# First sweep of a four-layer graph network: the additions to the adjacency tiles moved from VectorE to accumulating transfers

## The chip, the cores and the metric

The kernel runs on one core of a Trainium2 chip. The metric is the device time of one execution in microseconds. A profile comes from one further execution of the same program, in which the hardware profiler records every instruction and every transfer.

## The reference

`x` has 2708 rows of 512 features, `adj` is 2708 x 2708 with about 1% of random positive entries and a filled diagonal. Four layers, each followed by a layer norm of `x + layer(x)`:

```python
# layer 0: row-normalised mask added to the adjacency
mask = adj > 0
head = mask / max(sqrt(sum(mask*mask, -1)), 1e-12)
inc = adj + head
y0 = (inc @ x) / sum(inc, -1)
# layer 1: attention on the adjacency, and a plain graph convolution, each with a gate
x_a = softmax-like(exp(-leaky(s_left + s_right)) where adj != 0) @ (x @ W_sa)
y1 = sigmoid(attn_a * x_a + attn_b * (adj @ (x @ W_gcnb) + b))
# layer 2: x@w0 + A x@w1 + A A x@w2 + A A A x@w3
# layer 3: relu((a_norm @ x + x) @ W + b)
```

The change concerns layer 0 alone: `inc = adj + mask / sqrt(degree)`, element by element.

## The kernel before

All arithmetic is in fp32 on the transposed adjacency `adjT`, so that a tile has 128 source nodes as partitions and up to 384 target nodes as columns. The matrix is seen as 2 x 2 quadrants of 1354 rows ("11", "12", "21", "22"), and products with it are formed by a seven-product scheme: sums of quadrants (`comb`, L403, in place or into a tile `s3`) and sums of feature blocks (`x_sums`, `x_last`) go into seven matmul groups P1 to P7 (`step`, L458) instead of eight.

A sweep passes over all target columns once. There are seven, begun at `S[0]` to `S[6]`; the first one, `S[0]`, is layer 0. It takes its columns in four ranges, `RANGES0 = [(768, 256), (0, 384), (384, 384), (1024, 330)]` (start and width within a half). The first of them is "plain", with eight products and no sums of quadrants. The three later ranges are what the diff calls later. In each range 40 tiles of 128 rows (10 for each quadrant) and four tiles of the rest come in: for each half a tile `r` of 116 partitions (74 rows of the first half, 42 of the second) and a tile `r32` of 128 partitions, which holds the last 32 rows four times.

For each tile of the first sweep `prepare` or `rest_prepare` calls `prep0` before the tile is used. `prep0` has two VectorE instructions: L769 writes `t = (a > 0) * row`, with `row` the inverse roots of the degrees of this range's columns, spread over all partitions; L770 adds `t` to `a`. After that `comb` forms the sums of quadrants, `add_run` (L765) adds up the row sums that divide the result at the end, and the matmuls read the tiles.

`row` must be known before a range begins. So while one range runs, the tiles of the next are read a first time (`count_load`, L698 into tiles `cl`; its transfers carry L149 and L151, the lines of `move`), turned into 0/1 masks by ScalarE (`count_mask`, L712, L713), and added up by small matmuls (`count_tile`, L723). These first reads are issued by POOL's queue, except those of the range (0, 384), which SyncE issues. POOL's queue also stores the finished rows of the layer (`store`) and loads the next sweep's features, and POOL computes the reciprocal root of each layer norm (L560). The tiles themselves are loaded by SyncE (`load`, L394).

Buffers: adjacency tiles, the products `t` (the profile calls them s) and `s3` share one ring of `RING = 38` buffers; `tmp` has 17, from which `cl`, `row` and the sums come; masks have 6.

The order of the work is a list of (position, function) pairs, put in with `at` and sorted by position. A range is seven units long; for a range that begins at `pb`, quadrant 11 is loaded from `pb - 1`, 21 from `pb - 0.4`, 22 from `pb + 0.75`, 12 from `pb + 3.2`, and `prep0` follows each load by 0.3 units or more:

```python
when = {"11": (-1.0, 1.0), "21": (-0.4, 1.0), "22": (0.75, 0.8), "12": (3.2, 1.0)}
cw = {"s3": 0.3, "s1": 1.25, "s2": 2.1, "s4": 4.3}
pw = {ij: (p + 0.3, f) for ij, (p, f) in when.items()}
```

From the sorted list the framework's planner gives each engine its order of instructions, with costs of its own, and assigns buffers as they come free in its plan. The list's order is pinned on the engines at the beginning (positions under `START = 5.0`) and for the pieces put in with `hold`. Each engine, and each engine's transfer queue, then works strictly in its order, waiting on semaphores.

Of the kernel before, what the change touches and what calls it, by code (L numbers as in the profile page):

```python
# [24 lines left out]
ALU = mybir.AluOpType  # L25
# [5 lines left out]
RANGES0 = [(768, 256), (0, 384), (384, 384), (1024, 330)]  # L31
# [37 lines left out]
def gnn_kernel(ctx: ExitStack, tc: tile.TileContext, x, adjT, w_sa, a_sa, w_gcn, b_gcn, wab, bab, w_hop, w_out,  # L69
               b_out, out):  # L70
    nc = tc.nc
# [87 lines left out]
    def trans(nm):  # L159
        return pool.tile([P, 384], F32, name=nm, tag="ring", bufs=RING)  # L160
# [606 lines left out]
    def prep0(R0, n, h, col, w, a):  # L767
        t = trans("s")
        nc.vector.scalar_tensor_tensor(t[:w, :n], a[:w, :n], 0.0, row[R0, h][:w, :n], ALU.is_gt, ALU.mult)  # L769
        nc.vector.tensor_tensor(a[:w, :n], a[:w, :n], t[:w, :n], ALU.add)  # L770

    def run_sums(R0, n, h, after):

# [82 lines left out]
    for k in range(KW):  # L856
# [6 lines left out]
        at(7.5 + f, lambda k=k: x_last(k))  # L863
    at(9.3, start0)
    sweep(S[0], RANGES0, prep=prep0, extra=extra0, done=done0, first=True, sums=True)


# [510 lines left out]
    for i in range(4):  # L1378
        for g, p in enumerate((S[2] + 19.3 + 1.1 * i, S[3] + 6.6 + 1.3 * i)):
            a = ({}, g, i // 2, i % 2)  # L1380
# [220 lines left out]
```

## Time and profile before

| | |
|---|---|
| median of 3 runs | 2888.12 us (2884.0 to 2891.57) |
| the profiled execution | 2883.33 us, of which 2881.2 us are its span |
| TensorE busy | 2832.7 us, 98% of the span |
| VectorE busy | 2195.9 us, 76% |
| ScalarE, POOL busy | 550.1 us, 617.6 us |
| TensorE's granted clock | 0.998 of full speed |
| L769, mask times inverse root | 132 in the later ranges, 67.3 us |
| L770, the addition | 132 in the later ranges, 67.6 us; the last at 393.1 us |
| transfers | 510.04 MB, 177 GB/s over the span |

Times are counted from the start of the span. The later ranges' tiles are prepared between 103 and 394 us. An fp32 matmul leaves two records in the trace, one after the other; the records of TensorE are pipelined and their ends are modelled, so a row of TensorE that is full says that it was never seen empty. In a table by stages each engine has its busy time and the number of its instructions, and at the end stand TensorE's granted clock, the busy share of the 16 DMA engines and the GB/s that they moved. In the issue lists a queue with the name software_dynamic is POOL's.

### The profile page before, as it was taken

The page shows a single profiled execution, that of the slowest core. Times are in us where ns is not written, and L with a number is a line of the kernel's source. Part 1 is how long each engine was busy: PE and PEld are TensorE (multiplying, and loading weights), DVE is VectorE, ACT ScalarE, POOL GpSimd, SP SyncE. Part 2 cuts the span into 40 slices and gives each one's busy share as a digit, 9 for nine tenths or more (in the row PEclk, how much of TensorE's full clock was granted, in tenths as well). Part 3 has the DMA queues.
Part 4 walks back from the last instruction along what each step waited for, and adds up shares of the span by engine and source line. Part 5 has one row for each costly group of instructions (what it writes and reads, how often), then busy time and mean ns, then how long its engine had stood idle before and what let it go on. Part 6 is the DMA issues. An engine that isn't in the chain of part 4 may idle for free. (4 is left out here: it accounts for less than half of the span.)

```text
span 2881.2 us, 37482 instructions
## 1 busy us (share of the span) xinstructions
PE 2832.7 (98%) x10963; PEld 1870.3 (65%) x10963; DVE 2195.9 (76%) x5670; ACT 550.1 (19%) x1119; POOL 617.6 (21%) x1113
## 2 busy tenths in 40 slices
PE   7999999999999999999999999999999999999998
PEld 5655665657765656866666666666666666666665
DVE  6898798576736464654699787887878877799987
ACT  4544200111136444542100000000000100100001
POOL 0123223123320101122203123031230211501202
PEclk9999999999999999999999999999999999999999
DMA  7665466354544333565667767566675666754542
GB/s 229 193 212 179 133 204 218 124 181 143 183 140 130 117 113 98 151 198 151 195 205 236 213 192 246 166 201 208 187 250 168 181 197 182 230 174 145 175 142 92
DMA packets 368524, 510.04 MB, mean 177 GB/s; under 512 B 63424, under 2 KB 321700, under 8 KB 368320
## 3 DMA queue, kind: packets, MB, share of 16 engines
q1 hardware_dynamic: 302392, 370.56, 43.5%
q0 software_dynamic: 49344, 126.38, 13.1%
q10 hardware_dynamic: 16584, 10.71, 1.3%
q8 instruction: 87, 1.43, 0.2%
q14 instruction: 117, 0.96, 0.1%
HBM read 423.77 MB, written 83.65 MB: 176 GB/s over the span
## 5 line engine op out<-in xcount | busy, mean ns | idle before, releaser
L1212 DVE TENSOR_TENSOR z<-z 128x339 f32<-128x339 f32 (+1 forms) x966 | 454.3, 503 | 12.5 <-PE accu L1267 3.2
L1285 ACT COPY q<-accu 128x338 f32<-128x338 f32 (+1 forms) x84 | 34.6, 443 | 1003.3 <-PE accu L1267 806.0
L560 POOL TENSOR_TENSOR rstd<-rstd,neg_half 128x1 f32<-128x1 f32 (+3 forms) x91 | 59.3, 652 | 762.2 <-DVE rstd L559 516.6
L1267 PE MATMUL accc<-s,t 128*128 128x338 f32 (+1 forms) x644 | 198.1, 450 | 0.0
L1267 PE MATMUL accu<-z,t 128*128 128x338 f32 (+1 forms) x644 | 194.0, 448 | 1.5 <-DVE z L1212 1.5
L1267 PE MATMUL accd<-z,t 128*128 128x338 f32 (+1 forms) x644 | 193.9, 448 | 0.6 <-DVE q L1349 0.6
L1267 PE MATMUL accc<-z,t 128*128 128x338 f32 (+1 forms) x644 | 193.5, 448 | 0.5 <-ACT q L1285 0.5
L1400 POOL DMA_DIRECT2D Y<-y x192 | 105.1, 554 | 366.3 <-DVE y L1395 333.3
L403 DVE TENSOR_TENSOR a<-a,a 128x384 f32<-128x384 f32 (+2 forms) x330 | 162.4, 510 | 23.1 <-PE accu L458 22.4
L1267 PEld LDWEIGHTS accc<-s,t 128*128 128x128 f32 x644 | 120.9, 190 | 64.1 <-issue 7.5
L1267 PEld LDWEIGHTS accc<-z,t 128*128 128x128 f32 x644 | 122.0, 190 | 61.6 <-issue 1.0
L1267 PEld LDWEIGHTS accu<-z,t 128*128 128x128 f32 x644 | 121.7, 190 | 61.7 <-DVE z L1212 2.0
L1267 PEld LDWEIGHTS accd<-z,t 128*128 128x128 f32 x644 | 121.9, 190 | 60.5 <-DVE q L1349 1.5
L1212 DVE TENSOR_TENSOR s<-z 128x338 f32<-128x338 f32 (+1 forms) x322 | 149.7, 503 | 12.7 <-PE accc L1267 8.4
L1291 DVE TENSOR_TENSOR q<-q,accd 128x338 f32<-128x338 f32 (+1 forms) x112 | 56.0, 500 | 115.2 <-PE accd L1267 115.2
L1068 DVE SCALAR_TENSOR_TENSOR a<-a,e 128x384 f32<-128x384 f32 (+2 forms) x160 | 77.4, 507 | 49.8 <-ACT e L1067 49.5
L1066 ACT ACTIVATE e<-row,s_right 128x384 f32<-128x384 f32 (+5 forms) x176 | 96.3, 569 | 76.2 <-PE accc L458 20.4
L965 DVE SCALAR_TENSOR_TENSOR deg<-a,deg 128x384 f32<-128x384 f32 (+2 forms) x152 | 75.2, 505 | 19.0 <-DMA a<-in_adjT 17.9
L406 POOL DMA_DIRECT2D As<-a x120 | 64.9, 544 | 82.3 <-DVE a L403 80.3
L1067 ACT ACTIVATE e<-e 128x384 f32<-128x384 f32 (+5 forms) x176 | 79.3, 477 | 1.8
L606 PE MATMUL ps_d<-w,xT 128*128 128x512 f32 (+1 forms) x176 | 79.2, 593 | 0.4 <-ACT xT L597 0.4
L769 DVE SCALAR_TENSOR_TENSOR s<-a,row 128x384 f32<-128x384 f32 (+2 forms) x152 | 75.0, 505 | 6.0 <-ACT row L754 6.0
(683 smaller groups left out, 5869.0 us busy)
## 6 DMA issues: line engine op xcount, KB each, us to landing
z<-As SPq DMA_DIRECT2D x320, 169.5 KB
z<-As SPq DMA_DIRECT2D x320, 169.0 KB
a<-in_adjT SPq DMA_DIRECT2D x240, 192.0 KB
z<-in_adjT SPq DMA_DIRECT2D x240, 169.5 KB
z<-in_adjT SPq DMA_DIRECT2D x240, 169.0 KB
a<-in_adjT SPq DMA_DIRECT2D x120, 165.0 KB
a<-in_adjT SPq DMA_DIRECT2D x112, 128.0 KB
As<-a POOLq DMA_DIRECT2D x60, 192.0 KB, 4.2
```

What stands on the lines that cost most here:

```text
L403: nc.vector.tensor_tensor(A[r, dst, k][:, :n], A[r, a, k][:, :n], A[r, b, k][:, :n], op)
L406: nc.gpsimd.dma_start(out=SD[m][k * P : (k + 1) * P, R0 : R0 + n], in_=A[r, dst, k][:, :n])
L560: nc.gpsimd.tensor_tensor(rstd[:w, 1:2], rstd[:w, 0:1], neg_half[:w], ALU.pow)
L606: nc.tensor.matmul(o, lhs(c), r, start=c == 0 and n == 0, stop=c == DC - 1, skip_group_check=True)
L769: nc.vector.scalar_tensor_tensor(t[:w, :n], a[:w, :n], 0.0, row[R0, h][:w, :n], ALU.is_gt, ALU.mult)
L965: nc.vector.scalar_tensor_tensor(d[:w, :n], a[:w, :n], 0.0, d[:w, :n], ALU.not_equal, ALU.add)
L1066: nc.scalar.activation(e[:w, :n], row[R0, h][:w, :n], AF.Prelu, bias=s_right[:w, t : t + 1], alpha=0.01)
L1067: nc.scalar.activation(e[:w, :n], e[:w, :n], AF.Exp, scale=-1.0)
L1068: nc.vector.scalar_tensor_tensor(a[:w, :n], a[:w, :n], 0.0, e[:w, :n], ALU.not_equal, ALU.mult)
L1212: nc.vector.tensor_tensor(d[:, :n], Z[x + (k,)][:, :n], Z[y + (k,)][:, :n], op)
L1267: nc.tensor.matmul(B[home][:, :n], stat(v, k), a[:, :n], start=bool(start and k == 0), stop=k == nk - 1, skip_group_check=True)
L1400: nc.gpsimd.dma_start(out=rows[:, :, f * P : (f + 1) * P], in_=o[32 * f : 32 * (f + 1), : m * P].rearrange("p (b d) -> p b d", d=P))
```

## The change

In the first range everything stays as it was. In the three later ranges VectorE still computes the product `t`, but the addition to the adjacency tile is done by a transfer from `t` to `a`, both in on-chip memory, whose DMA engines add to what the destination holds. POOL issues it. A tile whose number of partitions is not a multiple of 16 (the rest tile of 116) is moved in two transfers, of 112 and of 4 partitions. The framework puts in the waits: the transfer waits for the product, and every reader of the tile, and the next owner of the buffer of `t`, wait for the transfer's landing.

```diff
     def prep0(R0, n, h, col, w, a):
         t = trans("s")
         nc.vector.scalar_tensor_tensor(t[:w, :n], a[:w, :n], 0.0, row[R0, h][:w, :n], ALU.is_gt, ALU.mult)
-        nc.vector.tensor_tensor(a[:w, :n], a[:w, :n], t[:w, :n], ALU.add)
+        if R0 == RANGES0[0][0]:
+            nc.vector.tensor_tensor(a[:w, :n], a[:w, :n], t[:w, :n], ALU.add)
+            return
+        c = w - w % 16
+        for r0, r1 in ((0, c), (c, w)) if c < w else ((0, w),):
+            nc.gpsimd.dma_start(out=a[r0:r1, :n], in_=t[r0:r1, :n], accum_op=ALU.add)
```

## The prediction

> **What bounds the kernel now.** I read the page's engine table first. The second fence, a table by stages of the first sweep's later ranges (us busy of each engine, granted TensorE clock, share of the 16 DMA engines, GB/s), then shows the place of the change.
>
> ```profile
> PE 2832.7 (98%) x10963; PEld 1870.3 (65%) x10963; DVE 2195.9 (76%) x5670; ACT 550.1 (19%) x1119; POOL 617.6 (21%) x1113
> ```
>
> ```profile
> 121.00:166.00 45.00, 45.00 (x204) 26.65 (x203) 44.05 (x107) 27.10 (x61) 18.56 (x33) 1.00 0.76 235
> 166.00:200.00 34.00, 34.00 (x150) 19.84 (x149) 32.73 (x84) 13.61 (x31) 6.47 (x12) 1.00 0.57 176
> 235.00:275.00 40.00, 40.00 (x178) 23.62 (x177) 38.54 (x89) 19.40 (x42) 18.43 (x32) 1.00 0.70 213
> 275.00:300.00 25.00, 25.00 (x111) 14.57 (x110) 24.34 (x58) 13.25 (x30) 6.49 (x12) 1.00 0.51 141
> 335.00:376.00 41.00, 39.37 (x145) 25.65 (x144) 38.62 (x97) 4.20 (x8) 12.22 (x22) 1.00 0.56 161
> 376.00:395.00 19.00, 19.00 (x69) 13.05 (x70) 18.97 (x47) 0.87 (x2) 0.00 (x0) 1.00 0.48 145
> 98.00:395.00 297.00, 295.37 (x1321) 183.79 (x1320) 255.82 (x644) 112.64 (x245) 78.45 (x140) 1.00 0.58 177
> ```
>
> TensorE is full in all of these stages, at full clock. VectorE is full too in the first six (94 to 100%), so this sweep is close to having two bounds; ScalarE, POOL and the DMA engines have room on average. A busy PE need not be PE at its peak, so the timeline of TensorE comes next: four records of 384 columns and three of the small counting matmuls repeat every 1.45 us, with nothing idle named between them.
>
> ```profile
> 151.23 1.54 PE L458 MATMUL accd<-a,T1A 128*128 128x384 f32 x4
> 152.60 0.22 PE L723 MATMUL cnt<-ones_bf,mask 128*128 128x1 bf16 x3
> ```
>
> Then the list of TensorE's waits from 98 to 395 us. It has this line alone (us in total, times, longest):
>
> ```profile
> PE accd L458 <- DVE a L403: 1.6, 3, 1.1
> ```
>
> So VectorE's load costs TensorE almost nothing today. Where it does is told by VectorE's timeline: mask product (L769), addition (L770), then soon the sum of two quadrants (L403), for which TensorE stands ready. Both timelines of 370 to 376 us, VectorE's and TensorE's:
>
> ```profile
> 371.17 0.50 DVE L770 TENSOR_TENSOR a<-a,s 128x330 f32<-128x330 f32 x1
> ...
> 371.99 0.50 DVE L769 SCALAR_TENSOR_TENSOR s<-a,row 128x330 f32<-128x330 f32 x1
> 372.40 0.50 DVE L403 TENSOR_TENSOR a<-a,a 128x330 f32<-128x330 f32 x1
> 372.82 0.50 DVE L770 TENSOR_TENSOR a<-a,s 128x330 f32<-128x330 f32 x1
> ...
> 374.05 0.50 DVE L403 TENSOR_TENSOR a<-a,a 128x330 f32<-128x330 f32 x1
> ```
>
> ```profile
> 372.96 1.38 PE L458 MATMUL accd<-a,T1C 128*128 128x330 f32 x4 [0.27 <-DVE a L403]
> ```
>
> Additions and sums alternate, one for one; the L403 at 374.05 reads the tile of the addition at 371.17, 2.4 us after its end, and TensorE takes each sum at once, with 0.27 us of waiting per tile. That is the narrowest place: a finished tile may come a few us later only if VectorE itself is earlier.
>
> **What the Trainium skill says.** "DMA: Bandwidth & Descriptors", SWDGE vs HWDGE vs iDMA: an accumulating transfer can only be issued by GpSimd, and transfers from all issuing engines share the same 16 DMA engines. The trace fits: POOL's and SP's queues together make up the share above. Same page, Anatomy of one DMA: a fixed 2.0 us and bytes over 436 GB/s, so 2.45 us for 192 KB. The trace has 4.2 to 5.3 us from POOL's issue to landing for 192 KB, so I use the trace. "Collectives: The Full Stack", The bandwidth ceiling: an addition in the DMA engine needs two source reads, and the measured rates differ by 1.93. No run here shows it yet.
>
> **The change part by part.** *Removed:* the L770 additions of three ranges, 44 each (40 tiles, 4 of the rest), 132 in all; the table of L770 by stages gives
>
> ```profile
> 98.00:395.00 297.00, 67.59 (x132) 1.00 0.58 177
> ```
>
> 67.6 us of VectorE. By stage it is 13.3 us in 121 to 166, 9.2 in 235 to 275, 12.4 in 335 to 376. What TensorE gets back is at most its waits on VectorE (1.6 us, and 3.6 us of the weight loads on the same sums, overlapping): 3 us. The rest is beside TensorE's own work.
>
> *Added on POOL:* a rest tile of 116 partitions makes two transfers (112 and 4), the others one: 40 + 2 x (2 + 1) = 46 a range, 138 in all. A direct transfer holds POOL 544 ns (L149 cl): 75 us beside 78 us in 297, so POOL itself is not full. If writing a third descriptor made it 0.8 us, 110 us would still fit. I cost POOL's time at nothing; its cover is its idle 219 us.
>
> *Added on the DMA engines:* 40 x 192 KB and 732 KB of rest for each of two ranges, 40 x 165 and 629 KB for the third: 24.6 MB. Price of a copy from POOL's own queue in this window:
>
> ```profile
> q0 software_dynamic: 6944, 21.24, 22.6%
> ```
>
> 21.24 MB took 22.6% of 297 us, 67 us, so 316 GB/s. 24.6 MB are 78 us at the price of a copy, 156 us with two reads. Below a copy it cannot be (it reads and writes at least as much); above two reads nothing excludes it. I take two reads, since the skill has that measured, and keep the copy as one bound and twice my value as the other. Against room, share by share: 0.58 x 297 = 172 us are used, so 250 (84%) or 328 (110%) of 297.
> By stage, with 0.59 us a tile as a copy (0.52 in the last range) and 1.18 (1.04) with two reads:
> - 121 to 166: 34.2 used + 25 tiles x 1.18 = 63.7 in 45: 18.7 over (as a copy 4 over)
> - 235 to 275: 28.0 + 17 x 1.18 = 48.1 in 40: 8.1 over
> - 275 to 300: 12.8 + 13 x 1.18 = 28.1 in 25: 3.1 over
> - 335 to 376: 23.0 + 26 x 1.04 = 50.0 in 41: 9.0 over
> - 376 to 395: 9.1 + 12 x 1.04 = 21.6 in 19: 2.6 over
> - 166 to 200: 19.4 + 12 x 1.18 = 33.6 in 34: full
>
> 41 us over. The emptier stretches (0.39 to 0.45 from 200 to 250 and 300 to 350) can take what is not due, such as counting loads and loads ahead. I take one third as moved there: 27 us remain on TensorE's path.
>
> *The added wait.* From the end of L769 to a finished tile, 0.54 us of addition becomes: POOL's turn, 0.55 us of issue, landing. POOL's turn is not free, since POOL issues in order and stands before counting loads:
>
> ```profile
> POOL cl L149 <- ACT mask L712: 70.6, 29, 19.1
> ```
>
> 2.4 us a time; I take 1. Landing: 5.3 us as the counting loads in 121 to 166, and 0.6 for the second read. In all 7.5 us (low 5, high 15). Behind the waiting L403 on VectorE stand further mask products and running sums, and TensorE behind those. The cover is the time taken off VectorE, 9 to 13 us in each of the three stretches, which lets the L769 run that much ahead where their tiles have landed. So I cost the latency at nothing while the DMA engines keep up.
> *Moved:* a product tile s keeps its ring buffer 7 us longer. 44 of those in about 100 us are 3 of 38 buffers. The SP queue's waits say who holds the loads:
>
> ```profile
> SPq L394 <- DVE a L770: 66.3, 27, 5.9
> ```
>
> Those 27 loads will wait for a landing instead. Three buffers of 38 are some 3 us less lead, inside the 7 us and more between a load's issue and its L769: nothing. Also late by what POOL waits for L769: the counting loads and the rstd power (L560), for which VectorE stands; again VectorE's freed time covers it. The planner will order all engines anew with its own costs; I hold that at zero, 5 us either way.
>
> **Sum.** -3 + 27 + 2 (at the start of each range VectorE has no lead yet, so part of one latency shows) = +26 us. The profiled execution took 2883.3 us (span 2881.2 and 2.1 around it), so 2909; the median of the runs shown, 2888.1, stands 4.8 above it, so 2914.
>
> **The rivals.** *The transfer costs no more than a copy* (27%). Then only 4 us are over in one stage, and the time freed on VectorE covers the latency: +0 to +8, about 2890. For it: the average share stays at 84%. Against: 0.9 and over is reached within 145 to 170 already.
> *Not slower, by VectorE's lead* (8%). In the three stretches before the L403 sums, 13.3, 9.2 and 12.4 us come off VectorE. If landing stays under about 9 us and DMA share under 1, the sums come earlier than today and TensorE's 3 us and some start-up waits vanish: 2883. It cannot be much more, since TensorE is full; it decides from a latency of 9 us downwards.
> *Pile-up* (18%). The addition costs the DMA engines four copies, or POOL's queue stands behind blocked counting loads for several us each time. At four copies the same table gives 312 us of additions and 172 of today in 297, 187 over; with the same third moved and a part lost to idle queues, +60 to +125, about 2975.
> *That the transfers don't replace the additions* I exclude: the line is conditioned on the range alone.
>
> **How the numbers follow.** Likeliest (47%): 2914, with 2898 to 2940 of its own. From 2884 to 2975 all cases but half of the pile-up and the better end of the second rival are in. A measurement of this kernel tells about 0.3%, 8.7 us, from no change. Faster by more than that: 6%. Within: the copy price and part of the second rival, 27%. Slower: 67%.
>
> **What would show it.** Right: the table by stages with DMA share over 0.9 in 121 to 166 and 235 to 275, TensorE with new waits on VectorE's L403 or on the counts, VectorE 67 us less busy, and accumulating packets that take about twice a copy's time. Wrong: DMA share near 0.8 with packets at a copy's price (first rival), or TensorE without waits and the sums earlier (second), or landings of 15 us and more (third).

## The result

The changed kernel takes **2978.1 us** (median of 4 runs, 2976.5 to 2978.8); the kernel before takes 2886.5 beside it (4 runs, 2884.0 to 2891.6). The ratio is **1.0314**, 95% interval 1.0296 to 1.0332: 92 us slower. The forecast was 2914, with a range up to 2975. The direction was right, the size was not.

The page's engine table after:

```profile
PE 2859.8 (96%) x10963; PEld 1879.4 (63%) x10963; DVE 2145.2 (72%) x5538; ACT 551.9 (19%) x1119; POOL 736.5 (25%) x1251
```

VectorE is 51 us less busy, POOL 119 us busier, and the span is 2976.5 instead of 2881.2 us. The additions that left VectorE add up to 67.6 us, but the records of its instructions overlap: the prediction's lines at 372.40 and 372.82 start 0.42 us apart and last 0.50, and busy time counts an overlap once. The table by stages (columns as in the prediction: time and length, busy us of TensorE, its weight loads, VectorE, ScalarE, POOL, then granted clock, DMA share, GB/s) shows where:

```profile
98.00:485.00 387.00, 321.45 (x1322) 194.22 (x1321) 211.31 (x526) 113.73 (x243) 198.92 (x278) 0.92 0.85 203
...
100.00:150.00 50.00, 45.29 (x217) 30.01 (x215) 30.18 (x87) 17.13 (x39) 24.23 (x33) 0.97 0.98 239
150.00:200.00 50.00, 33.59 (x128) 18.03 (x128) 31.76 (x77) 21.67 (x46) 30.77 (x44) 0.85 0.95 221
...
350.00:400.00 50.00, 50.00 (x234) 29.71 (x233) 23.24 (x62) 16.69 (x34) 17.02 (x29) 1.00 0.58 150
400.00:450.00 50.00, 38.98 (x128) 24.62 (x126) 27.21 (x66) 3.75 (x7) 32.09 (x45) 0.86 0.90 195
```

The first row covers the same work of TensorE as 98 to 395 us of before (1322 matmul records against 1321). It now lasts 387 us instead of 297: these 90 us are nearly the whole difference, 95 us between the two spans. In it neither TensorE nor VectorE is full any more. VectorE was 86% busy there and is 55%; the DMA engines went from 0.58 to 0.85.

TensorE's waits of the first 620 us (us in total, times, longest):

```profile
PE pr L751 <- DVE r L743: 25.6, 5, 13.7
PE cnt L723 <- ACT mask L713: 22.1, 12, 5.8
PE accd L458 <- DVE a L403: 18.1, 10, 3.0
PE cnt L723 <- DVE mask L710: 11.3, 13, 3.9
```

The fourth row belongs to the first range and is what it was (11.2). The third was 1.6 us, as the prediction shows. The first two were, before:

```profile
PE pr L751 <- DVE r L743: 5.8, 3, 2.7
PE cnt L723 <- ACT mask L713: 3.8, 6, 2.0
```

So the next range's rows cost 20 us more, its counts 18, the sums of quadrants 21 and 22 16.5. With the other small rows it is some 61 us.

VectorE's waits, below them those of SyncE's queue, and last those of ScalarE, before and after, say what stands behind:

```profile
DVE s L403 <- DMA a<-s: 38.4, 21, 4.6
DVE s L769 <- DMA a<-s: 29.5, 14, 6.9
DVE a L403 <- DMA a<-s: 23.4, 17, 3.7
DVE s L769 <- issue: 16.7, 5, 5.6
```

```profile
SPq L394 <- DMA a<-s: 178.9, 43, 15.9
```

```profile
ACT mask L712 <- DMA cl<-in_adjT: 10.2, 5, 4.8
```

```profile
ACT mask L712 <- DMA cl<-in_adjT: 89.4, 28, 14.3
```

`DMA a<-s` is the landing of an accumulating transfer. VectorE stands 91 us for it: the sums (L403) for a finished tile, the products (L769) for a buffer. SyncE's loads wait 179 us for it, since product and tile keep their ring buffers until the landing; before, they waited 66 us for L770. ScalarE waits 89 us for counting reads that come late.

The transfers themselves, from the page's groups (busy us, mean ns, idle before) and its list of issues (KB, median us to landing):

```profile
L775 POOL DMA_DIRECT2D a<-s x120 | 111.4, 1257 | 133.4 <-DVE s L769 56.2
```

```profile
a<-s POOLq DMA_DIRECT2D x80, 192.0 KB, 5.4
```

An issue holds POOL 1257 ns on average, and from issue to landing a tile of 192 KB takes 5.4 us (median). POOL's queue on the page (packets, MB, share of 16 engines' span), before and after:

```profile
q0 software_dynamic: 49344, 126.38, 13.1%
```

```profile
q0 software_dynamic: 68448, 151.02, 18.0%
```

13.1% of 2881.2 us are 377 us, 18.0% of 2976.5 are 536: the added 24.64 MB take 158 us.

**One stall, followed to its end.** TensorE's longest wait, 13.67 us, is for the transposes that spread the next range's row. The counts were complete at about 325 us. VectorE's timeline (start, duration; in brackets the idle time before and what ended it) shows why L735, which reads them, came at 340.69:

```profile
325.50 1.17 DVE L769 SCALAR_TENSOR_TENSOR s<-a,row 128x384 f32<-128x384 f32 x2 [5.36 <-DMA a<-in_adjT]
...
330.21 0.56 DVE L769 SCALAR_TENSOR_TENSOR s<-a,row 128x384 f32<-128x384 f32 x1 [1.87 <-DMA a<-s]
...
335.96 0.56 DVE L769 SCALAR_TENSOR_TENSOR s<-a,row 128x384 f32<-128x384 f32 x1 [1.88 <-issue]
...
338.33 0.56 DVE L769 SCALAR_TENSOR_TENSOR s<-a,row 128x384 f32<-128x384 f32 x1 [1.34 <-DMA r<-s]
...
340.69 0.28 DVE L735 TENSOR_SCALAR r<-cnt 128x1 f32<-128x1 f32 x3
```

Ahead of it, in order, stand products of quadrant 12, waiting for late loads or for landings. None of that work needs the counts; they only stand behind it. On TensorE:

```profile
342.50 0.78 PE L751 MATMUL pr<-ident,r 128*128 128x128 f32 x3 [13.67 <-DVE r L743]
343.07 2.82 PE L458 MATMUL accu<-a,T2C 128*128 128x384 f32 x4
```

The four records at 343.07 take 2.82 us. Four records of this size took 1.54 in the timeline of before (at 151.23, in the prediction). The table in steps of 2 us tells why; the third column from the end is the granted clock, the next one the DMA share:

```profile
330.00:332.00 2.00, 0.00 (x0) 0.00 (x0) 1.03 (x2) 0.00 (x0) 0.70 (x2) 1.00 1.09 174
332.00:334.00 2.00, 0.00 (x0) 0.00 (x0) 1.87 (x4) 0.00 (x0) 2.00 (x4) 0.52 1.06 214
...
342.00:344.00 2.00, 1.50 (x5) 1.23 (x6) 1.29 (x4) 0.43 (x1) 1.16 (x3) 0.50 1.10 234
344.00:346.00 2.00, 2.00 (x5) 1.02 (x4) 0.57 (x2) 0.31 (x1) 0.10 (x1) 0.57 1.03 344
346.00:348.00 2.00, 2.00 (x10) 1.19 (x9) 1.05 (x2) 1.12 (x3) 2.00 (x4) 1.00 0.67 172
```

By the means of these rows the clock falls to half at about 332.1, 3.3 us after the last matmul (328.8), and is back at about 345.7, 3.2 us after work resumes. The Trainium skill has this in "TensorE: Matmul & The Clock Gate", Part 1: half rate after an idle window of some 3.4 us, full rate after a busy one as long. This stall agrees.

Other falls of the clock in the same trace come after shorter pauses. TensorE started no matmul between 148.47, where the last one ended, and 151.10, which is 2.6 us, and the clock is at half from about 151.2:

```profile
148.00:150.00 2.00, 0.47 (x2) 0.00 (x0) 1.02 (x4) 0.74 (x2) 1.53 (x3) 1.00 0.82 227
150.00:152.00 2.00, 0.90 (x5) 0.60 (x6) 0.00 (x0) 1.94 (x5) 1.89 (x3) 0.79 0.94 191
152.00:154.00 2.00, 2.00 (x7) 0.91 (x6) 0.00 (x0) 0.01 (x1) 0.00 (x0) 0.50 0.67 191
```

All spells at half clock in this trace, but for the last, which the end cuts off, take 3.41 us or a multiple of it. If the time is cut into these steps of 3.41 us, the clock falls 12 times, each time after a step in which TensorE has a matmul for at most 0.46 of the time. After steps with 0.47 or more it never falls. So, other than the page has it, an empty 3.4 us was not needed here: a step that was less than about half busy was enough. The border is an estimate, since the ends of matmul records are modelled; in the other runs' traces it lies between 0.43 and 0.52, with one fall after 0.65.

The rows of 2 us also show DMA shares above 1.00 (1.10 from 342 to 344). Packets' times overlap in the records, so a share of 1.00 is not a ceiling.

How much of the 92 us is the half clock? I take the starts of TensorE's matmul records from 90 to 620 us and subtract from each distance the time of such a matmul at full clock (0.32 us for 384 columns). The remainder is 20.7 us before and 109.7 after. Gaps over 0.6 us, true waits, grew by 64 (15.2 to 79.6), remainders of 0.1 to 0.6 us by 22 (6.6 to 29.1). Among the latter are 57 matmuls with a remainder of 0.25 to 0.35 us, a half clock's worth; before there is one at most. So an estimated **20 us of the 92 are matmuls at half clock**, a loss that follows from the waits.

### The profile page after: what moved, and what is told of

Its sections match the earlier page's. It is cut to its first block, busy times and chain, and to the rows that moved or that the text cites. A ratio compares the mean times of both kernels' runs of the same rounds, so it can differ in the third digit from the quotient of the medians.

```text
span 2976.5 us, 37750 instructions
## 1 busy us (share of the span) xinstructions
PE 2859.8 (96%) x10963; PEld 1879.4 (63%) x10963; DVE 2145.2 (72%) x5538; ACT 551.9 (19%) x1119; POOL 736.5 (25%) x1251
## 5 line engine op out<-in xcount | busy, mean ns | idle before, releaser
L403 DVE TENSOR_TENSOR a<-a,a 128x384 f32<-128x384 f32 (+2 forms) x330 | 163.3, 511 | 47.0 <-DMA a<-s 23.4
L775 POOL DMA_DIRECT2D a<-s x120 | 111.4, 1257 | 133.4 <-DVE s L769 56.2
L769 DVE SCALAR_TENSOR_TENSOR s<-a,row 128x384 f32<-128x384 f32 (+2 forms) x152 | 74.9, 509 | 63.1 <-DMA a<-s 29.5
L403 DVE TENSOR_TENSOR s<-a,a 128x384 f32<-128x384 f32 (+2 forms) x110 | 54.7, 513 | 63.4 <-DMA a<-s 38.4
L712 ACT ACTIVATE mask<-cl 128x384 bf16<-128x384 f32 (+3 forms) x132 | 65.6, 500 | 106.9 <-DMA cl<-in_adjT 89.4
```

What stands on the lines that cost most here:

```text
L403: nc.vector.tensor_tensor(A[r, dst, k][:, :n], A[r, a, k][:, :n], A[r, b, k][:, :n], op)
L712: nc.scalar.activation(m[:w, :n], t[:w, :n], AF.Sign)
L775: nc.gpsimd.dma_start(out=a[r0:r1, :n], in_=t[r0:r1, :n], accum_op=ALU.add)
```

## The experiments

All are compared with the kernel before on the same chip; "+" is the difference of medians. The expectations name their theories by letters. L: the latency of a landing. T: traffic on the DMA engines. O: the planner's new order. P: POOL's queue. Later ones: C, counts and rows behind VectorE carry the loss, and S, late sums do. V: the written order of VectorE, and R, the ring's buffers being held. A and M: traffic counts in full by itself, or mostly through longer landings.

**e1_cols48: the first eighth of the columns alone.** 

```diff
-        nc.gpsimd.dma_start(out=a[r0:r1, :n], in_=t[r0:r1, :n], accum_op=ALU.add)
+        m = n // 8
+        nc.gpsimd.dma_start(out=a[r0:r1, :m], in_=t[r0:r1, :m], accum_op=ALU.add)
```

> Only the first eighth of the columns is added (48 or 41 of a tile); the rest of the addition is left out. Every transfer, every wait and POOL's 138 issues stay, the bytes of the additions fall to an eighth. Theory T (the DMA engines' 152 us of added packet time is what TensorE sees): nearly all of the loss is gone, 2886 + 5 to 15 us. Theory L (readers wait in order on VectorE for a landing, about 5.4 us instead of 0.54 us, and the bytes matter only through it): [...]about half of the loss stays, 2920 to 2945 us, with VectorE still waiting for a<-s in its list of waits.

Measured 2937.6, +54.8, ratio 1.0191 (1.0176 to 1.0207); 3.4 us to land for the full tiles. This is L's figure. Every row is still a packet, so an eighth of the bytes is a third of the added packet time: POOL's queue has 14.6% of 2938.2 us, 429, against 377 before, so 52 of the 158 us are added. With this third, 60% of the loss is there. T alone cannot be it.

**e2_copy: the whole tile as a plain copy.**

```diff
-        nc.gpsimd.dma_start(out=a[r0:r1, :n], in_=t[r0:r1, :n], accum_op=ALU.add)
+        nc.gpsimd.dma_start(out=a[r0:r1, :n], in_=t[r0:r1, :n])
```

> The transfer overwrites the tile with the product instead of adding to it (the addition is left out); instruction order on all engines, transfers and waits are those of the changed kernel. The DMA engines read once instead of twice: added packet time near 75 us instead of 152. Theory T: the loss is halved or better, 2905 to 2925 us. Theory L: landing falls by about 1 us of 5.4, so most stays, 2945 to 2965 us.

Measured 2928.5, +45.7, ratio 1.0163 (1.0146 to 1.018); 3.7 us to land for 192 KB, 539 ns of POOL per issue. This lies between the two expectations. It is also a measurement of the prediction's first rival, which gave +0 to +8 for transfers at the price of a copy: that was wrong by some 40 us.

**e3_only12, e4_only2122, e5_rest: the transfers for some tiles alone** (quadrant 12; quadrants 21 and 22; all but 21 and 22). The condition in `prep0`, with VectorE adding where it holds:

```diff
-        if R0 == RANGES0[0][0]:
+        if R0 == RANGES0[0][0] or not (h == 0 and KT <= col < NT):    # e3
+        if R0 == RANGES0[0][0] or not (h == 1 and col < NT):          # e4
+        if R0 == RANGES0[0][0] or h == 1 and col < NT:                # e5
```

> Only the tiles of quadrant 12 are added by transfers (30 of 132), all others by VectorE as before. Before the change their first reader came 6 to 11 us after the addition, so a landing of 5.4 us fits. Theory L: no loss, 2884 to 2892 us. Theory T: a share of the loss like the share of bytes, 23% of 92 us, 2900 to 2912 us.

> Only the tiles of quadrants 21 and 22 are added by transfers (60 of 132); their first reader came 0.03 to 6.6 us after the addition before the change. Theory L: nearly the whole loss, 2955 to 2985 us. Theory T: 45% of the loss, 2922 to 2935 us.

> The complement of the kernel with quadrants 21 and 22 by transfers: here quadrants 11, 12 and the rest tiles (72 of 132) go by transfers, 21 and 22 are added by VectorE. TensorE's order of instructions is that of the changed kernel. Theory L (waits for landings in front of the sums of 21 and 22): small, 2888 to 2905 us. Theory T (added packet time, here 55%): 2926 to 2938 us. Theory O (the planner's new order of TensorE's instructions costs the time, whatever the transfers do): 2960 us and more.

Measured: quadrant 12 alone 2891.2, +8.4, 1.0027 (1.0016 to 1.0038); quadrants 21 and 22 2932.4, +49.6, 1.0178 (1.0162 to 1.0193); the others 2911.2, +26.9, 1.0093 (1.0078 to 1.0108). In the written order, the product of a tile of 22 stands 0.2 units ahead of the sum that needs it (1.05 and 1.25), that of quadrant 12 0.8 ahead (3.5 and 4.3). For each transfer that is 0.28 us in e3 (30 transfers) and 0.83 in e4 (60): it costs most where the reader stands close behind. L has its figure in e3 but not in e4, which gives the figure of T; e5 lies between the two. The parts e4 and e5 make 76.5 of the 92 us. TensorE's order in e5 is that of the kernel after, at less than a third of its loss, so O falls as the main cause: the order costs at most e5's 27 us.

**e6_load_alone: VectorE adds, and POOL copies the row twice per tile into buffers that nothing reads.**

```diff
+        nc.vector.tensor_tensor(a[:w, :n], a[:w, :n], t[:w, :n], ALU.add)
...
-        nc.gpsimd.dma_start(out=a[r0:r1, :n], in_=t[r0:r1, :n], accum_op=ALU.add)
+        for _ in range(2):
...
+            nc.gpsimd.dma_start(out=z[:, :n], in_=row[R0, h][:, :n])
```

> VectorE adds all tiles as before, and for each of the 132 tiles POOL issues two plain copies of the row tile into unused buffers that nobody reads: about as much packet time as the additions (two copies for one addition), more issues on POOL (two of 0.54 us for one of 0.84 us and more), no reader that waits. Theory L: 2884 to 2895 us. Theory T: most of the loss, 2940 to 2980 us.

Measured 2946.1, +61.8, ratio 1.0216 (1.0201 to 1.0231). That is T's figure. L expected nearly nothing and falls as the only cause. But POOL's queue stood still here too, each copy waiting for the one before in its buffer:

```profile
POOL dump L782 <- DMA dump<-row: 49.7, 52, 4.2
```

So this run shows traffic together with a blocked POOL.

**e7_counts_on_sync: all counting reads issued by SyncE.**

```diff
-        move(nc.sync if R0 == RANGES0[1][0] else nc.gpsimd, t[:w, :n], adjT[...])
+        move(nc.sync, t[:w, :n], adjT[...])
```

> The changed kernel with all counting loads issued by SyncE's queue, none by POOL's; all else as in the changed kernel. Theory P (POOL's queue, where transfers and counting loads stand behind one another, delays both): 25 us or more come back, 2920 to 2955 us. Theory L: a few us at most, 2968 to 2982 us; slower is possible, since SyncE's queue then holds the tile loads behind counting loads.

Measured 2969.1, +84.8, ratio 1.0296 (1.0281 to 1.0311). 7 us of the 92 come back, where P asked for 25 and more; L's figure holds. ScalarE's wait for counting reads falls from 89 to 42 us, so about half of it came from POOL's queue. The 7 us are a net gain, since in SyncE's queue the counting reads stand ahead of tile loads.

**e8_early: quadrants 21 and 22 loaded and prepared earlier.**

```diff
             when = {"11": (-1.0, 1.0), "21": (-0.4, 1.0), "22": (0.75, 0.8), "12": (3.2, 1.0)}
+            if first:
+                when["21"], when["22"] = (-0.63, 1.0), (0.25, 0.8)
```

> The changed kernel with quadrant 21 loaded and prepared 0.23 units (some 3 us) earlier in the list, and quadrant 22 0.5 units (some 7 us) earlier, in the three later ranges. Theory L: more room between product and sum, a third to two thirds of the loss comes back, 2915 to 2950 us. If the ring of buffers or VectorE's order leaves no room for it, nothing changes, 2965 to 2985 us. Theory T: nothing changes.

Measured 2970.8, +86.5, ratio 1.0299 (1.0281 to 1.0316). The waits moved instead of going: the next rows cost TensorE 31.9 us, the tiles s3 18.7. Little changes, as the expectation has it where the ring or VectorE's order leaves no room, and for T.

**e9_last_range: the transfers in the last range alone.**

```diff
-        if R0 == RANGES0[0][0]:
+        if R0 != RANGES0[3][0]:
```

> Accumulating transfers in the last range (R0 1024) alone; VectorE adds in the two ranges before it. Behind the last range's tiles stand no rows and no counts of a range to come, only the sums of quadrants 21/22. If the loss is made mostly through counts and rows standing behind VectorE's waits (theory C), this range gives little: 0 to +10 us (2883 to 2894). If it is made mostly through the sums arriving late for TensorE's own products (theory S), the last range gives a third or so of the 92 us: +22 to +35 (2906 to 2919), with TensorE's wait for the sums of L403 above 6 us.

Measured 2910.4, +25.0, ratio 1.0089 (1.0074 to 1.0104). TensorE's wait for the sums:

```profile
PE accd L458 <- DVE a L403: 13.1, 6, 3.4
```

A range with no rows and no counts to prepare loses more than a quarter of the 92 us, so these are not needed for the loss. S has its figure.

**e10_nocount_before and e11_nocount_after: the counting of the next ranges left out of both kernels.** Reads, masks, counts and rows go; the row is a constant.

```diff
-                for i in range(NT):
-                    q = pb + p + d * i / NT
-                    at(q - 0.7, lambda i=i, h=h: count_load(R1, n1, h, i))
-                    at(q - 0.35, lambda i=i, h=h: count_mask(R1, n1, h, i))
-                    at(q, lambda i=i, h=h: count_tile(R1, n1, h, i))
-                at(pb + p + d, lambda h=h: count_row(R1, n1, h))
-                at(pb + p + d + 0.15, lambda h=h: spread_row(R1, n1, h))
+                at(pb + p + d + 0.15, lambda h=h: fixed_row(R1, n1, h))   # memset of row[R1, h]
```

> The kernel before, with the counting of the ranges to come left out: their reads of the adjacency, masks, column counts, inverse roots and rows; the row is a constant filled in by VectorE. It is the base for the next run. TensorE loses its 11 us of column counts and most of its waits for them: 2868 to 2878 by every theory.

> The kernel after with the same counting left out, row constant. Against the run before it: theory C (counts and rows carry the loss) gives +10 to +35 us, since nothing that comes from VectorE, ScalarE or a counting transfer stands between ranges any more. Theory S (late sums) keeps +60 to +90 us. Leaving out the counting also takes its reads off the DMA engines, so a drop can be C or traffic; a figure that stays refutes both.

Measured 2861.6 (ratio to the kernel before 0.9921, 0.9905 to 0.9938) and 2932.3 (1.0168, 1.0153 to 1.0183). The base gained more than expected, 24 us. Between the two are **70.7 us**: counts and rows, which hold 38 us of the added named waits, are worth 21, with the DMA engines' relief from their reads included. That is S's figure, not C's. Take them away and TensorE waits for the next thing behind VectorE:

```profile
PE accd L458 <- DVE a L403: 21.9, 11, 6.1
PE ps_n L589 <- DVE P1c L519: 13.7, 3, 9.5
PE rs L787 <- DVE run L769: 13.3, 4, 4.0
```

These are the sums, the results of the half range (L519) and the running sums of the divisor. A row of waits names who comes last, not what the time is lost to.

**e12_load_half: e6 with one copy per tile** instead of two.

> VectorE adds, as before, and beside each sum one plain copy of the row tile into an unused buffer by POOL, nothing waiting for it: half of the traffic of the run with two copies per tile. The theory of traffic (busy DMA engines make loads and counts late) gives +15 to +35 us (2899 to 2919). If the run with two copies was slow mostly because POOL's queue was full (its dumps waited for one another), one copy leaves POOL free and gives 0 to +8 (2884 to 2892).

Measured 2919.6, +34.3, ratio 1.0127 (1.0111 to 1.0142), at the upper end of the theory of traffic. POOL's queue still waited for its own copies (22.5 us), and VectorE 37 us for the rstd power behind them (10 before), so this too is an upper bound for traffic alone.

**e13_sums_later, e14_own_buffers, e16_later_and_own.** Later: the sums of 21 and 22 stand a quarter unit later. Own: four of six products get buffers outside the ring. Then both.

```diff
-            cw = {"s3": 0.3, "s1": 1.25, "s2": 2.1, "s4": 4.3}
+            cw = {"s3": 0.3, "s1": 1.5 if first else 1.25, "s2": 2.1, "s4": 4.3}      # e13, e16
...
-        t = trans("s")
+        turn[0] += 1                                                                  # e14, e16
+        i = turn[0] % 6 if R0 != RANGES0[0][0] else 5
+        t = feat.tile([P, D], F32, name="s", tag=f"w_{i}") if i < 4 else trans("s")
```

> The kernel after, with the sums of quadrants 21 and 22 placed a quarter of a phase later (1.5 instead of 1.25), so that the product of a tile stands 0.45 phases ahead of the sum that needs it instead of 0.2; a phase is about 16 us here, so 3.3 us become 7.4, against a median of 5.3 us to land and 1.3 us to issue. Theory V (VectorE's list is written for a sum that is ready at once; it stands still in each landing) gives a third to two thirds back: 2915 to 2948. Theory R (the buffers of the ring held until landing make loads and products late) gives little back, 0 to 15 us: 2963 to 2978.

> The kernel after, with four of six products in buffers of their own outside the ring (those that hold weights at other times), so that the ring keeps its 38 buffers for loads and sums. Theory R gives a third to two thirds back: 2915 to 2948, and SyncE's waits for the landing of s fall from 179 us to under 70. Theory V gives 0 to 15 us back: 2963 to 2978.

> Both edits at once, later sums and own buffers. If V and R are two separate parts the gains add up: with the two figures of this call g1 and g2 the time is 2978 minus their sum within 10 us. If both only make up for the same saturated transfers (theory of traffic), the time stays above 2935, since the DMA engines still have the same 536 us of work.

Measured 2966.6, +82.3, ratio 1.029 (1.0274 to 1.0305); 2961.6, +77.4, 1.0275 (1.0258 to 1.0292); 2961.6, +77.4, 1.0272 (1.0257 to 1.0288). Of the 92 us they give back 9, 14 and 14, each known to some 4 us. Together they give no more than own buffers alone, and each is far from the third that V or R asked for. Later sums only moved VectorE's waits for landings: 47 instead of 62 us stand at the sums, but 42 instead of 29.5 at the products. SyncE's queue with own buffers:

```profile
SPq L394 <- DMA a<-s: 148.9, 24, 15.0
```

It still waits 149 us for landings, and the DMA share is 0.96 to 1.03 in three of the stages of 50 us (150 to 250, 300 to 350). More room before the sums, or more buffers, did not help much. That this is because the transfers themselves are late under such load is likely, but no run here separates it.

**e15_rows16: only the first 16 rows of each tile.**

```diff
-        c = w - w % 16
-        for r0, r1 in ((0, c), (c, w)) if c < w else ((0, w),):
-            nc.gpsimd.dma_start(out=a[r0:r1, :n], in_=t[r0:r1, :n], accum_op=ALU.add)
+        nc.gpsimd.dma_start(out=a[:16, :n], in_=t[:16, :n], accum_op=ALU.add)
```

> Only the first 16 rows of each tile are accumulated (the other rows get no product): 16 packets per tile instead of 128, so nearly no traffic, and the shortest way from issue to landing that such a transfer has. Theory V without any traffic: the landing stays at 2 us or above and gives +30 to +50 us (2914 to 2935), as the copies did. If traffic makes the greater part of it, +5 to +20 (2889 to 2905).

Measured 2920.1, +35.9, ratio 1.0129 (1.0114 to 1.0144), within V's figure. The stretch in the table by stages, of this kernel and then of e2_copy:

```profile
98.00:440.00 342.00, 312.06 (x1358) 191.14 (x1356) 214.59 (x538) 115.46 (x245) 183.33 (x272) 0.98 0.62 170
```

```profile
98.00:440.00 342.00, 311.68 (x1338) 190.76 (x1337) 211.04 (x528) 114.57 (x245) 150.49 (x278) 0.96 0.73 230
```

With an eighth of the bytes and a fifth of the added packet time (14.0% of 2919.0 us are 409, 32 more than before), the DMA engines nearly as free as before (0.62 against 0.58) and 3.3 us to land, 36 us are lost. That is the price of a landing where there was none, with POOL's issue of 1140 ns in front of it. It is not sharp: e1, with as few bytes but 128 packets for a tile and an issue of 1434 ns, lost 55. The copy of the whole tile costs 10 more, and from copy to change, with the second read, the smaller packets and the longer issues, it is another 46.

**e17_traffic_apart, e18_traffic_apart_nocount: the change's very transfers beside VectorE's additions**, from the row into six buffers that nothing reads; e18 without counting.

```diff
+        nc.vector.tensor_tensor(a[:w, :n], a[:w, :n], t[:w, :n], ALU.add)
...
-            nc.gpsimd.dma_start(out=a[r0:r1, :n], in_=t[r0:r1, :n], accum_op=ALU.add)
+            nc.gpsimd.dma_start(out=z[r0:r1, :n], in_=row[R0, h][r0:r1, :n], accum_op=ALU.add)
```

> VectorE adds, as before; beside each sum POOL issues the very accumulating transfer of the kernel after (same bytes, same packets, same time on POOL), but from the row into one of six buffers that nothing reads. Traffic and POOL's time stay, the waits for the landing and the ring's buffers go. Theory A (two causes that add up: the sixteen-row run with hardly any traffic gave 36 us, so traffic is the other 56): +46 to +66 us (2930 to 2950), TensorE waiting for counts above all. Theory M (traffic mostly makes landings longer, and costs little where nothing waits for them): +15 to +38 (2899 to 2922).

> The same with the counting of the ranges to come left out, constant rows; its base is the kernel before without counting, 2861.6 us. If the traffic bites through the counting alone (late counting reads, late masks), +0 to +10 us (2862 to 2872). If it bites through the tiles' own loads as well, +20 to +45 (2882 to 2907). With the 71 us of the kernel after without counting, the first would make all of the 71 the work of the landings.

Measured 2973.3, +90.1, ratio 1.0307 (1.029 to 1.0323), and 2950.0, +88.4 over e10. Both are above every figure expected. VectorE's and TensorE's waits in e17:

```profile
DVE rstd L562 <- POOL rstd L560: 75.2, 16, 15.8
```

```profile
PE cnt L723 <- ACT mask L713: 36.0, 12, 16.8
```

The second row, with ScalarE's wait for counting reads behind it (90.3 us, as in the kernel after), is not the DMA engines' load alone: e15 has 48 us of ScalarE's wait at a share of 0.62, and e7 took half of it away. The first, 10 us before and 14 after, is not in the change: POOL's in-order queue held the layer norm's power behind transfers that waited for their buffers. So neither A nor M is decided: 90 is an upper bound for traffic and POOL together, and e18, with 81 us of the same wait for POOL, tells more of POOL's queue than of traffic. How much full traffic costs where nothing at all waits for it stays open.

## Why the prediction was wrong

**The load of the DMA engines: right.** It foretold 156 us for the additions and 328 us of engine time in the stretch. Measured are 158 us, and 0.85 of 387 us, which are 329. The two reads that the Trainium skill speaks of ("Collectives: The Full Stack", The bandwidth ceiling) fit: 158 us are 2.0 times the 78 of a copy, and 2.1 times the 74 that the copies of e2 added (15.4% of 2924.3 us, less 377). In the records a row of 1536 bytes is a packet of its own that takes 140 ns (median), while POOL's copies put three rows into a packet of 178 ns, 59 a row; the few copies of a single such row in the kernel before took 65 ns. The runs show this ratio, not its reason.

**The step from load to time: wrong.** It added up what exceeded a full engine stage by stage, 41 us, moved a third, and laid 27 on TensorE's path. For that the engines would have to run at 1.0 wherever work is due, and 1.0 would have to be their most. They were at 0.85 over the stretch, where 329 us of work took 387, and at most at 0.98 in a stage of 50 us; the rows of 2 us go above 1.0. In-order queues issue this work, and they waited for buffers, landings and VectorE, as their waits show; that these queues set the 0.85 is argued, not shown. In place of the 27 us the runs have 46 from copy to change, and 56 from sixteen rows to all. These are not traffic alone: on the same steps the landing grows from 3.7 and 3.3 to 5.4 us, and from the copy POOL's issue from 539 to 1257 ns.

**The latency at nothing: wrong, by 36 us in e15, 55 in e1.** The size of the landing was about right: 5.9 us foretold, 5.4 measured. (The 2.45 us for 192 KB that the prediction worked out, and rightly set aside, are an estimate; e2's copies took 3.7.) What failed is the cover named, VectorE's freed time. Freed time is not a lead. VectorE's list stays in the order planned: a product, soon after it the sum of a tile whose landing is 5.4 us away. It waits there, 91 us in all, and with it all that is behind. It was idle for 45% of the stretch. That more distance to the sum alone would cure this is not shown: e13 gave 9 us back. 36 and 56 are the 92 us, as e15 splits them; e1 would split them into 55 and 37. Some 20 of the 92 are TensorE at half clock, which no step of the sum held.

**The ring at nothing: wrong, but small.** The estimate of three buffers priced only their number. SyncE waits 179 us for landings, and own buffers give 14 back.

**Smaller terms.** The 3 us of waits to be won back did not come. The 2 us for the starts of the ranges stand against 20 us of added waits for the next row; leaving rows and counts out altogether is worth 21. POOL's time was put at nothing, with issues of 0.54 to 0.8 us: they took 1.26 us, and POOL is busy for 199 of the 387 us. For the counting reads alone its queue cost 7 us net (e7); what it cost the additions themselves was not separated. The planner's order, held at nothing, costs 27 us at most (e5).

**The rivals.** The price of a copy fell by the packets, and its +0 to +8 by e2's 45.7. VectorE's lead fell although its conditions were met in the mean: a landing of 5.4 us, under its 9, and a share of 0.85. The pile-up had the right time, 2975, for other reasons: the transfers cost two copies, not four. Its point, POOL and the transfers standing in each other's way, is nearest to what e17 shows.

The best of the tried placements of the transfers, quadrant 12 alone, is 8.4 us slower than the kernel before. Little could have been won: by the first fence of the prediction TensorE was 98% busy, and VectorE's additions lay beside its work.

## What to carry to other kernels

When an operation goes from an in-order engine to a transfer, look first at how far behind it its first reader stands in that engine's written order: if that is less than issue and landing together, the engine stands still, however much busy time was taken off it. Free share on the DMA engines does not tell that added work will fit: here the sum came out right, and the stretch was 90 us longer at a share of 0.85. And where TensorE will now wait, add what its clock costs after the gaps, the short ones too.

## What the hardware showed unexpectedly

- The clock fell to half in steps of 3.41 us, after each step in which TensorE was busy for 0.46 of the time or less, so after pauses of 2.6 us too. In the longest stall it came back 3.2 us after work had resumed. This was about a fifth of the loss.
- An accumulating transfer's issue holds POOL about as long for 16 rows (1140 ns) as for 128 (1257), and twice as long as a copy's (539 ns).
- From issue to landing it was 3.3 us for 16 rows of 1536 bytes, 3.4 for 128 rows of 192 bytes, and 5.4 for the whole tile, each beside the kernel's other transfers.
- A row of 1536 bytes was one packet of 140 ns when it was added, and 65 ns when a single row was copied.
